# Reordering ScalarE's queue in a fused graph-attention kernel: exp behind the copy of the next transposed weights, part of the norms moved to the attention phase, projection and v adjacent

## Chip, cores and metric

One core of one Trainium2 chip. The metric is the time on the device of one execution, in microseconds (us); each kernel was run several times and the median is quoted. Engines are named as in the profile: PE is TensorE (PEld its weight loads), DVE VectorE, ACT ScalarE, POOL GpSimd, SP SyncE.

## The reference, cut to what matters

The input x is 128 batches of 128 nodes by 512 features, in float32; `adj` is one 128 × 128 matrix used as convolution weight and as attention mask.

```python
# layer 0 (W1 = W2 = adj, so C - A is only b)
A = einsum('od,bdn->bon', adj, x)
pre = A[:, :, None, :] + (C - A)[:, :, :, None]
x = layernorm(x + max(relu(pre), axis=-1))
# layer 1: 8 heads of 64
q, k, v = split(x @ w_qkv)
attn = softmax(where(adj == 0, -inf, q @ k.T * 64**-0.5))
o = (attn @ v) @ w_proj + b_proj
x = layernorm(x + o + layernorm(o) * ln_gamma + ln_beta)
```

## The kernel before

The 128 batches go in 32 groups of 4. A group passes through two phases. In the **dense phase** PE makes eight pieces of qkT for the whole group (pieces 4 to 11, twelve matmuls and 2.8 us each, since a float32 product is made of three products of rounded parts), with one projection left over from the group before among them, and then v of its first batch. In the **attention phase** there are four slots, one for each batch. In a slot PE transposes the weights of the group before (ppt), makes the scores of this group (psc), transposes x of the next group (ptx), applies the transposed weights to v (pav), projects, makes another v and convolves x of a later group (pa).

All of it is a list of pairs (place in time, function). Sorted by place, the list gives the order of PE and of ACT by hand; DVE, POOL and the transfers are ordered by the scheduler. A place is therefore no time at which something happens. It only says which instruction is ahead of which in its engine's queue. The code is shortened: `...` marks what is left out, and conditions for the first and last groups are dropped.

```python
ps_1 = pool("ps_1", bufs=4, PSUM)   # 128 x 512 float32 each: ptx, pav, pm/pd, pa
ps_2 = pool("ps_2", bufs=2, PSUM)   # 128 x 1024 float32 each: pp, psc, ppt
...
STARTS = [0.0, 7.3, 17.4, 27.5, 34.8]

def normed(b, u, v, w, z):          # the norms of layer 1 for one batch
    at(u - 14.0, residual, b)       # xb <- x1, by DMA
    at(u - 10.0, residual_beta, b)  # xb += beta, accumulating DMA issued by POOL (L360)
    at(u - 4.0, residual_o, b)      # xb += o,    accumulating DMA issued by POOL (L380)
    at(u, stats, b, 1)              # ACT square (L392), POOL deviation (L398, L399)
    at(v, norm_1, b)                # DVE L412 (o = (o - mean) * gamma), then L385
    at(w, stats, b, 2)              # ACT square, POOL L398, L399, L406
    at(z, norm_2, b)                # ACT L420, then the output
...
    # attention(g, t, starts), one slot
    last(0.0, transpose_e); last(1.0, weights_T)     # ppt, and ACT's copy eT (L336)
    now(0.95, scores); now(2.1, masked); now(3.5, row_max); now(6.3, exps)
    nxt(2.0, transpose_x); nxt(2.5, split_x); nxt(3.3, split_high)
    u += 2.5
    if i and 0 < g:
        projection((g - 1) * G + i - 1, u); u += 2.8
    last(0.0, attend); last(1.0, heads); last(1.7, split_high of o); u += 1.0
    dense_step(g, i + 1, u)                          # v of the next batch
...
    # beside_dense(g, t): what runs beside the dense phase
    for i in range(G):
        at(u + 0.6 + 0.9 * i, add_0, b + i)          # layer 0 of the next group, ACT L186
        at(u + 5.0 + 0.9 * i, stats_0, b + i)
    at(u + 8.7, rstd_0, b, G)                        # POOL
    for i in range(G):
        at(u + 14.0 + 1.5 * i, norm_0, b + i)        # ACT L205
    for i in range(G):
        u = t + 1.0 + 4.5 * i
        normed((g - 2) * G + i, u, u + 3.0, u + 6.0, u + 9.0)
```

Line numbers: what the profile of the kernel before calls L392 (square), L398 and L399 (deviation) is L391, L397 and L398 after the change, and L388 (`nmean`, the negated mean) is L403. The sum of each qkT or v piece is an ACT copy of its main half (L280) and a DVE addition of its rest (L284). In the profile before, the accumulating DMA issues of 256 KB take 6.7 us (L360, from the beta row) and 3.3 us (L380, from o), medians from issue to landing.

Of the kernel before, what the change touches and what calls it, by code (L numbers as in the profile page):

```python
# [12 lines left out]
ALU = mybir.AluOpType  # L13
# [11 lines left out]
def tile_adj_resnorm_d2(  # L25
# [34 lines left out]
    nc = tc.nc  # L60
    B, T, D = x.shape
    P = 128
    assert T == P and D == 512 and B % 4 == 0
    G = 4
    NG = B // G
# [169 lines left out]
    def split_high(key):  # L235
        nc.scalar.copy(*hs.pop(key))  # L236
# [138 lines left out]
    def projected_rest(b):  # L375
        add_sum(b, 1, pps.pop(("o", b))[1], 1.0, os[b])
# [5 lines left out]
    def add_sum(b, n, in0, scalar, in1):  # L382

        s = sums_of[b, n] = small.tile([P, 3], FP, tag=f"sum{n}", name=f"sum{n}_{b}")
        nc.vector.scalar_tensor_tensor(  # L385
            os[b], in0, scalar, in1, op0=ALU.mult, op1=ALU.add, accum_out=s[:, 0:1],
        )
        nc.gpsimd.tensor_scalar(s[:, 2:3], s[:, 0:1], -1.0 / D, None, op0=ALU.mult)  # L388

    def squares(x, s):  # L390

        nc.scalar.activation(  # L392
            square, x, AF.Square, bias=s[:, 0:1], scale=-float(D), accum_out=s[:, 1:2],
        )

    def deviation(s, n):

        nc.gpsimd.tensor_scalar(s, s, float(D) ** -3, EPS, op0=ALU.mult, op1=ALU.add)  # L398
        nc.gpsimd.tensor_tensor(s, s, mhalf[:, :n], op=ALU.pow)  # L399

    def stats(b, n):
        s = sums_of[b, n]
        squares(os[b], s)  # L403
        deviation(s[:, 1:2], 1)
        if n == 2:
            nc.gpsimd.tensor_tensor(s[:, 2:3], s[:, 2:3], s[:, 1:2], op=ALU.mult)  # L406

    def norm_1(b):
        o, s, xb = os[b], sums_of.pop((b, 1)), xbs.pop(b)
        if b >= B - G:  # L410
            nc.vector.tensor_tensor(xb, xb, o, op=ALU.add)
        nc.vector.scalar_tensor_tensor(  # L412
            o, o, s[:, 2:3], gamma_sb, op0=ALU.add, op1=ALU.mult,
        )
        add_sum(b, 2, o, s[:, 1:2], xb)
# [10 lines left out]
    def at(place, f, *a):  # L426
        plan.append((place, len(plan), f, a))
# [3 lines left out]
    DENSE = (2 * KC + 2) * CHUNK  # L431
    PERIOD = DENSE + STARTS[-1]

    def normed(b, u, v, w, z):

        at(u - 14.0, residual, b)
        at(u - 10.0, residual_beta, b)
        at(u - 4.0, residual_o, b)
        at(u, stats, b, 1)
        at(v, norm_1, b)  # L440
        at(w, stats, b, 2)
        at(z, norm_2, b)

    def projection(b, u):
        at(u, project, b)
        at(u + 1.9, projected_main, b)
        at(u + 2.8, projected_rest, b)
        at(u - 5.0, bias, b)

    def attention(g, t, starts):  # L450

        for i in range(G):
            u = t + starts[i]
            now, last, nxt, far = (
                (lambda place, f, *a, k=k: at(u + place, f, (g + k) * G + i, *a))
                if 0 <= g + k < NG else (lambda *a: None)
                for k in (0, -1, 1, 2)
            )
            last(0.0, transpose_e)
            last(1.0, weights_T)  # L460
            now(0.95, scores)
            now(2.1, masked)
            now(3.5, row_max)
            now(6.3, exps)
            nxt(2.0, transpose_x)
            nxt(2.5, split_x)
            nxt(3.3, split_high)
            u += 2.5
            if i and 0 < g:
                projection((g - 1) * G + i - 1, u)  # L470
                u += 2.8
            last(0.0, attend)
            last(1.0, heads)
            last(1.7, lambda b: split_high(("o", b)))
            u += 1.0
            if 0 < g != NG - 1 and i < G - 1:
                dense_step(min(g, NG - 1), i + 1, u)
                u += 2.8
            far(-20.0, load_x)
            far(0.0, conv)  # L480
            far(1.0, conv_max)
            if NG - 1 <= g:
                v = u + 8.9 if g == NG else u + 12.5 + 2.0 * i
                normed((g - 1) * G + i, v, v + 1.5, v + 3.1, v + (8.6 if g == NG else 5.6))
                now(10.0, weights)

    def dense_step(g, j, u):
        at(u, dense, g, j)
        at(u + 1.9, dense_main, g, j)
        at(u + CHUNK, dense_rest, g, j)  # L490
# [5 lines left out]
    def beside_dense(g, t):  # L496

        if g + 1 < NG:
            b = (g + 1) * G
            u = t if g else t + 19.5  # L500
            at(u + 0.5, relu_0, b, G)
            for i in range(G):
                at(u + 0.6 + 0.9 * i, add_0, b + i)
                at(u + 5.0 + 0.9 * i, stats_0, b + i)
            at(u + 8.7, rstd_0, b, G)
            for i in range(G):
                at(u + 14.0 + 1.5 * i, norm_0, b + i)
                at(u + 15.0 + 1.5 * i, keep_0, b + i)
        for i in range(G):
            if g > 0:  # L510
                at(t + 6.0 + 3.0 * i, weights, (g - 1) * G + i)
            if g > 1:
                u = t + 1.0 + 4.5 * i
                normed((g - 2) * G + i, u, u + 3.0, u + 6.0, u + 9.0)


    for b in range(G):
        at(-20, load_x, b)
        u = -15 + 1.75 * b
# [23 lines left out]
    t = 0.0  # L543
    for g in range(NG):
        beside_dense(g, t)
        if g == 0:
            dense_steps(g, range(3 * KC), t)
            t += 3 * KC * CHUNK
            attention(g, t, (0.0, 4.5, 9.0, 13.5))
            t += 18.0  # L550
            continue
        chunks = [*range(G, 3 * KC)]
        dense_steps(g, chunks[:1], t)
        t += CHUNK
        if g > 1:
            projection((g - 1) * G - 1, t)
            t += CHUNK
        dense_steps(g, chunks[1:], t)
        t += len(chunks[1:]) * CHUNK
        if g < NG - 1:  # L560
            dense_step(g, 0, t)
            t += CHUNK
            attention(g, t, STARTS)
            t += STARTS[-1]
        else:

            attention(g, t, (0.0, 3.6, 10.0, 16.4))
            t += 22.8
            dense_step(g, 0, t)
            projection(g * G - 1, t + CHUNK)  # L570
            t += 2 * CHUNK
            attention(NG, t, (0.0, 6.0, 15.0, 24.0))
            projection(B - 1, t + 32.0)
# [35 lines left out]
```

## Time and profile before

| | before |
|---|---|
| median of three runs | 2138.18 us (2135.07 to 2140.66) |
| span of the profiled run | 2148.1 us |
| mean granted PE clock in it | 0.986 |
| PE waits psc for qkT | 50.0 us, 31 times: once in each of groups 2 to 30, twice in group 31 |
| period of a usual group (from its piece 4 to that of the next) | 65.2 us (median of groups 2 to 29); 66.9 to 67.5 in the six of them in which the clock was lower for a while |

How to read it: an engine that is 96% busy, as PE is here, sets the end, so only the places count where it stands still. The waits of PE give those places by the tile it wanted and the instruction that released it. From there one goes back along the timeline, from releaser to releaser, until an engine is found that did not wait for data but for its own order. The lines are in the prediction below.

### The profile page before, as it was taken

What the parts mean: (1) busy time and instruction counts of PE and PEld (TensorE: products, weight loads), DVE (VectorE), ACT (ScalarE), POOL (GpSimd) and SP (SyncE); (2) the same over time, 40 slices, a digit from 0 to 9 for tenths busy, and PEclk for the clock granted to TensorE, in tenths of its full rate; (3) what the DMA queues carried; (4) which work ended last, traced back from release to release, by engine and by line L of the source; (5) the groups of instructions that cost most, each with busy time, mean ns of one, the idle gap of its engine ahead of it and who ended that gap; (6) DMA issues with size and microseconds to landing.
All of it is one profiled execution on the core that took longest, in us unless ns stands there. A gap on an engine that the chain in (4) does not pass through costs nothing. (4 is left out here: it accounts for less than half of the span.)

```text
span 2148.1 us, 34985 instructions
## 1 busy us (share of the span) xinstructions
PE 2059.5 (96%) x12033; PEld 1602.7 (75%) x12033; DVE 1623.6 (76%) x2615; ACT 1453.9 (68%) x4130; POOL 640.8 (30%) x1329
## 2 busy tenths in 40 slices
PE   7899999999999999999999999999999999999987
PEld 5677777777777777777777777777777777777765
DVE  7788777787777887777877678876778777788767
ACT  5766676765776666767667666667676677666665
POOL 2122333322333222333223332223332233322335
PEclk8999999999999999999999999999999999999998
DMA  6224555334554345554345443454543455434444
GB/s 183 76 62 114 128 128 124 89 93 123 128 128 107 87 110 128 125 128 102 85 118 126 125 117 87 103 128 123 127 100 81 121 128 128 113 79 100 114 102 115
DMA packets 134434, 240.65 MB, mean 112 GB/s; under 512 B 14704, under 2 KB 18928, under 8 KB 134256
## 3 DMA queue, kind: packets, MB, share of 16 engines
q1 hardware_dynamic: 97680, 172.27, 26.3%
q0 software_dynamic: 36288, 66.08, 18.4%
q8 instruction: 95, 1.56, 0.3%
q14 instruction: 83, 0.68, 0.1%
q10 hardware_dynamic: 288, 0.07, 0.0%
HBM read 138.74 MB, written 67.11 MB: 96 GB/s over the span
## 5 line engine op out<-in xcount | busy, mean ns | idle before, releaser
L317 ACT ACTIVATE e<-e,nmax 128x128 f32<-128x128 f32 x1024 | 396.4, 389 | 47.5 <-DVE nmax L310 47.5
L388 POOL TENSOR_SCALAR sum<-sum 128x1 f32<-128x1 f32 x256 | 68.8, 269 | 1109.3 <-DVE o L385 1109.2
L420 ACT ACTIVATE o<-o,sum 128x512 f32<-128x512 f32 x128 | 104.2, 814 | 198.7 <-POOL sum L406 198.4
L236 ACT CAST x_h<-xh 128x512 fp32r<-128x512 f32 x128 | 79.3, 621 | 225.9 <-DVE xh L224 225.5
L399 POOL TENSOR_TENSOR sum<-sum,mhalf 128x1 f32<-128x1 f32 (+1 forms) x291 | 206.5, 710 | 24.1
L295 PE MATMUL psc<-qkT 64*128 64x128 f32 x2048 | 157.6, 288 | 50.0 <-DVE qkT L284 50.0
L336 ACT COPY eT<-ppt 128x1024 f32<-128x1024 f32 x128 | 128.9, 1007 | 100.9 <-PE ppt L332 100.9
L412 DVE SCALAR_TENSOR_TENSOR o<-o,sum,gamma_sb 128x512 f32<-128x512 f32 x128 | 97.0, 758 | 129.5 <-ACT square L392 123.9
L392 ACT ACTIVATE square<-o,sum 128x512 bf16<-128x512 f32 x256 | 182.5, 713 | 14.7 <-DVE o L385 12.8
L317 ACT ACTIVATION_READ_ACCUMULATOR e<-e,nmax 128x1 f32 x1024 | 192.1, 188 | 0.0
L295 PEld LDWEIGHTS psc<-qkT 64*128 64x128 f32 x2048 | 127.1, 187 | 79.2 <-DVE qkT L284 56.2
L385 DVE SCALAR_TENSOR_TENSOR o<-o,sum,xb 128x512 f32<-128x512 f32 x128 | 96.0, 750 | 107.0 <-POOL sum L399 106.8
L302 DVE SCALAR_TENSOR_TENSOR e<-psc,mask 128x1024 f32<-128x1024 f32 x128 | 156.2, 1220 | 13.7 <-PE psc L295 13.7
L332 PEld LDWEIGHTS ppt<-ident,e 128*128 128x128 f32 x1024 | 120.6, 142 | 51.7 <-issue 46.7
L326 DVE TENSOR_TENSOR e<-e,sums 128x1024 f32<-128x1024 f32 x128 | 155.9, 1219 | 1.0
L310 DVE TENSOR_REDUCE nmax<-e 128x8 f32<-128x1024 f32 x128 | 154.6, 1208 | 0.0
L360 POOL DMA_DIRECT2D xb<-in_L_gnn_ln_beta_dram x128 | 125.1, 981 | 82.8 <-DMA xb<-x 69.3
L345 PE MATMUL pav<-eT,v 128*64 128x128 f32 x2048 | 144.4, 285 | 1.1 <-ACT eT L336 1.1
L345 PEld LDWEIGHTS pav<-eT,v 128*64 128x64 f32 x2048 | 112.4, 139 | 42.0 <-issue 40.3
L398 POOL TENSOR_SCALAR sum<-sum 128x1 f32<-128x1 f32 (+1 forms) x291 | 90.4, 311 | 159.3 <-ACT square L392 144.5
L170 PE MATMUL pa<-xt,adjT 128*128 128x512 f32 x256 | 135.3, 615 | 0.4 <-DVE adjT L99 0.4
L332 PE MATMUL ppt<-ident,e 128*128 128x128 f32 x1024 | 133.7, 274 | 0.0
(4778 smaller groups left out, 5570.7 us busy)
## 6 DMA issues: line engine op xcount, KB each, us to landing
xt<-in_x_dram SPq DMA_DIRECT2D x128, 256.0 KB, 2.7
x<-xt SPq DMA_DIRECT2D x128, 256.0 KB, 3.7
xb<-x SPq DMA_DIRECT2D x128, 256.0 KB, 3.2
xb<-in_L_gnn_ln_beta_dram POOLq DMA_DIRECT2D x128, 256.0 KB, 6.7
o<-in_L_gnn_b_proj_dram SPq DMA_DIRECT2D x128, 256.0 KB, 3.7
out_dram<-o SPq DMA_DIRECT2D x128, 256.0 KB, 3.7
xb<-o POOLq DMA_DIRECT2D x124, 256.0 KB, 3.3
wraw<-in_L_gnn_w_qkv_dram SPq DMA_DIRECT2D x12, 256.0 KB, 4.4
```

What stands on the lines that cost most here:

```text
L170: nc.tensor.matmul(pa[b], adjT, xs[b], start=True, stop=True)
L295: nc.tensor.matmul(psc[:, s, hp, :], qkT[hs, hp, i, :], qkT[hs, KC + hp, i, :], start=True, stop=True,)
L302: nc.vector.scalar_tensor_tensor(e, pscs.pop(b).rearrange("p s a m -> p (s a) m"), scale, mask_b, op0=ALU.mult, op1=ALU.add,)
L310: nc.vector.tensor_reduce(nmax, es[b], AX.X, ALU.max, negate=True)
L317: nc.scalar.activation(e[:, j, :], e[:, j, :], AF.Exp, bias=nmax[:, j : j + 1], accum_out=sums[:, j : j + 1],)
L326: nc.vector.tensor_tensor(e, e, sums[:, :, None].to_broadcast([P, H, P]), op=ALU.mult)
L332: nc.tensor.transpose(ppts[b][:, j, :], e[:, j, :], ident)
L336: nc.scalar.copy(eTs[b], ppts.pop(b))
L345: nc.tensor.matmul(pavs[b][s * HD : (s + 1) * HD, hp, :], v[:, h * HD : (h + 1) * HD], eT[:, s * HP + hp, :], start=True, stop=True,)
L360: nc.gpsimd.dma_start(xbs[b], row(ln_beta), accum_op=ALU.add)
L392: nc.scalar.activation(square, x, AF.Square, bias=s[:, 0:1], scale=-float(D), accum_out=s[:, 1:2],)
L399: nc.gpsimd.tensor_tensor(s, s, mhalf[:, :n], op=ALU.pow)
```

## The change

The intent is to even out ACT's queue. There are five parts: (1) the small POOL operation `nmean` goes behind the square; (2) each batch's exp goes behind ACT's copy eT of the next slot; (3) attend goes ahead of the projection, so that projection and v are adjacent; (4) the layer-0 norms of the next group go later, two of the four into the attention phase; (5) the layer-1 norms are spread out, those of a group's fourth batch partly into the attention phase. ACT's small copies `split_high` shift a little with (2) and (3).

```diff
-        nc.gpsimd.tensor_scalar(s[:, 2:3], s[:, 0:1], -1.0 / D, None, op0=ALU.mult)   # in add_sum
...
         squares(os[b], s)                                                             # in stats
+        nc.gpsimd.tensor_scalar(s[:, 2:3], s[:, 0:1], -1.0 / D, None, op0=ALU.mult)
...
-            now(6.3, exps)
+            now((8.5, 11.3, 11.6, 9.0)[i] if 0 < g < NG - 1 else 6.3, exps)
-            nxt(3.3, split_high)
+            nxt(3.3 if i == 3 else 5.0, split_high)
             u += 2.5
+            if g < NG - 1:
+                last(0.0, attend)
+                u += 1.0
             if i and 0 < g:
                 projection((g - 1) * G + i - 1, u)
                 u += 2.8
-            last(0.0, attend)
-            last(1.0, heads)
-            last(1.7, lambda b: split_high(("o", b)))
-            u += 1.0
+            ... (the last groups keep the old place of attend)
+            last(0.1, heads)
+            last(0.8, lambda b: split_high(("o", b)))
...
             for i in range(G):
-                at(u + 0.6 + 0.9 * i, add_0, b + i)
-                at(u + 5.0 + 0.9 * i, stats_0, b + i)
-            at(u + 8.7, rstd_0, b, G)
+                v = u if g == 0 else u + 3.8
+                at(v + 0.6 + 0.9 * i, add_0, b + i)
+                at(v + 5.0 + 0.9 * i, stats_0, b + i)
+            at(u + 8.7 if g == 0 else u + 12.7, rstd_0, b, G)
             for i in range(G):
-                at(u + 14.0 + 1.5 * i, norm_0, b + i)
+                v = u + (14.0 + 1.5 * i if g == 0 else (17.0, 21.0, DENSE + 4.0, DENSE + 12.0)[i])
+                at(v, norm_0, b + i)
...                                                # keep_0 (a transfer) moves along
-                u = t + 1.0 + 4.5 * i
-                normed((g - 2) * G + i, u, u + 3.0, u + 6.0, u + 9.0)
+                u = t + (3.0, 7.5, 12.0, DENSE + 2.0 if g < NG - 1 else 16.0)[i]
+                normed((g - 2) * G + i, u, u + 3.5, u + 7.0, u + 10.5)
```

## The prediction

> **What bounds the kernel now.** I began with the page: busy time by engine, to see which engine can set the end.
>
> ```profile
> PE 2059.5 (96%) x12033; PEld 1602.7 (75%) x12033; DVE 1623.6 (76%) x2615; ACT 1453.9 (68%) x4130; POOL 640.8 (30%) x1329
> ```
>
> TensorE (PE) is busy 96%; only time in which it stands still can be won by reordering. So next I read who PE waited for (total us, times, longest us):
>
> ```profile
> PE psc L295 <- DVE qkT L284: 50.0, 31, 3.2
> PE ptx L216 <- ACT xt L205: 8.4, 4, 2.9
> PE pp_(1, 4)_699 L249 <- ACT x_h L236: 6.5, 1, 6.5
> ```
>
> One wait counts: 50.0 us in 31 pieces, one in each of groups 1 to 31 (the other rows are the start-up). The scores of a group's first batch wait for the last piece of qkT. Why it is late shows in the timeline around that place in group 15, from which I cut the lines that hold each other up:
>
> ```profile
> 1019.09 1.87 POOL L360 DMA_DIRECT2D xb<-in_L_gnn_ln_beta_dram  x2 [2.26 <-DMA xb<-x]
> ...
> 1021.94 0.19 POOL L406 TENSOR_TENSOR sum<-sum 128x1 f32<-128x1 f32 x1
> 1022.17 0.81 ACT L420 ACTIVATE o<-o,sum 128x512 f32<-128x512 f32 x1 [3.19 <-POOL sum L406]
> 1022.89 0.57 ACT L280 ACTIVATE qkT<-pm_(15, 11)_9737 128x512 f32<-128x512 f32 x1
> ...
> 1023.50 0.69 DVE L284 TENSOR_TENSOR qkT<-qkT,pd_(15, 11)_9738 128x512 f32<-128x512 f32 x1 [3.79 <-ACT qkT L280]
> ...
> 1024.24 0.49 PE L295 MATMUL psc<-qkT 64*128 64x128 f32 x4 [2.29 <-DVE qkT L284]
> ```
>
> Bottom up: PE waits for VectorE's sum, that for ScalarE's (ACT) copy, which stands behind the fourth batch's final norm (L420), which waits for GpSimd's (POOL) L406, which stands behind two DMA issues waiting for data. Matmuls of piece 11 had ended near 1017.3; ACT reached it 5.6 us later only by its order. The twelve score matmuls before the wait start at 1021.02; at .068 us each the other four were due at 1021.84, so 2.40 us is lost where the idle column says 2.29: loss is idle + 0.11.
>
> [...] ACT stood 3.19 us in front of L420 with a copy ready behind it. [...] Here it is order instead in the old gap; but buffers come into my second step. [...] a VectorE op of 0.68 us is followed 0.60 us later. I therefore add steps between starts, not durations. [...] the trace has 3.2 us from issue to landing for xb<-x, and I use that.
>
> **The change part by part.** Instructions and counts stay the same; only order moves. Built, the two programs have equal numbers of rows on every engine.
>
> *Removed: the late qkT.* In ACT's built order the fourth batch's statistics, final norm and two of four first norms (norm_0) leave the projection phase for the attention phase. Behind piece 10 stands only the third batch's final norm, then piece 11. I chained this by old durations from the start of the last attention slot (0). POOL issues the first beta DMA at 17.5 and, 5.3 us later (as 1001.98 to 1007.27), may go on: norm_0's statistics to 25.3, the next issue to 26.3, the third batch's first statistics to 27.3; so its L385 ends at 28.0, its buffer is loaded again by 31, issue to 32, and L398, L399, L406 (1.1 us) end at 33.1. Then L420 to 33.9, the copy of piece 11 to 34.4, VectorE's sum to 35.1. PE wants it at 37.4 (1057.50 - 1050.47 = 7.03 from the slot's start to the first piece, and 1021.84 - 991.49 = 30.35 from there to the scores). Slack 2.3 us. I take this wait as gone in groups 2 to 30: 45.2 us idle + 29 × 0.11 = 48 us back. Groups 1 and 31 held 1.2 and 3.6 us; part of it goes too, I say 3 us.
>
> *Added: VectorE in the first attention slot.* The built order puts L412 of the moved batch directly ahead of the masking of the first scores, in each of groups 2 to 29 that I sampled. L412 overwrites what the square reads, so it waits for the square; the square now stands in ACT's order behind the copy eT. And PE's second convolution matmul (pa, L170) needs the PSUM buffer that holds ptx until L226 has read it (four buffers, so the fourth allocation back). These steps are in the old timeline:
>
> ```profile
> 1024.78 1.23 DVE L302 SCALAR_TENSOR_TENSOR e<-psc,mask 128x1024 f32<-128x1024 f32 x1
> 1025.92 0.68 DVE L224 TENSOR_SCALAR xh<-ptx 128x512 int32<-128x512 int32 x1
> 1026.52 1.21 DVE L310 TENSOR_REDUCE nmax<-e 128x8 f32<-128x1024 f32 x1
> 1027.64 0.68 DVE L226 TENSOR_TENSOR x_l<-ptx,xh 128x512 fp32r<-128x512 f32 x1
> ...
> 1029.18 1.02 PE L170 MATMUL pa<-xt,adjT 128*128 128x512 f32 x2
> ```
>
> From the start of the transposes (ppt): eT starts at +1.13 (as at 1040.25 to 1041.38), square +2.14, L412 +2.98 (square's start + 0.84), mask +3.65, L224 +4.79, L310 +5.39, L226 +6.51, its end +7.19, pa +7.25. PE alone would be there at +6.6 (ptx +2.06, pav +2.65, pa 3.93 after pav as at 1025.25 to 1029.18). **New wait 0.65 us**.
>
> In the next slot VectorE is still behind: L227, the head split, L385 of the moved batch (+0.67), v and the maximum end at +11.38, so the mask starts there, and L226 ends at +14.92. The v matmul (pm) that reuses that ptx buffer was due at +14.57 (slot start 8.10 + 6.47, as 1030.03 to 1036.50). **New wait 0.40 us**. By the third slot VectorE is on time again (20.91 against 20.90). Sum 1.05 × 29 groups = 30 us given back.
>
> *Moved at no cost: attend ahead of the projection.* It needs eT at once, 0.5 us after it is ready instead of 3 us. With exp behind eT, ACT is free by then. Slot 1: the head's xh ends at +7.79, then oh, x_h and the v copy, some 0.5 each, end at 9.33, where the transposes end at 8.10 + 1.13 = 9.23. Slot 2: eT to 10.34, exp 3.08, square, norm_0, x_h and L420 to 16.2, oh and v to 18.4, against 19.85. Without the exp move the 3.08 us of exp would stand in front. The switch pauses of PE (0.17 us around pav) number two per slot in either order. *nmean moved on POOL* (0.2 us each, L388): beside other work; it takes POOL's head-of-line wait for VectorE off a few places.
>
> Sum: -48 - 3 + 30 = **-21 us**, 2138 - 21 = 2117 us, 1.0% faster.
>
> **The rivals.**
> 1. *All of it is won.* The new waits are too small to see: 2138 - 53 = 2085 us, 2.5% faster. For it: ACT and VectorE have idle time enough, 32% and 24%. Against: in the attention phase VectorE's work per slot adds to 9.6 of 10.2 us (mask 1.14, row maximum 1.12, weights 1.25, two splits 3.6, projection 1.28, v and maximum 1.2), and the L412 chain holds no estimate but old durations.
> 2. *The old wait stays, smaller.* POOL now takes its L380 ahead of the norm_0 statistics; L380 waits for the beta DMA (6.7 us to land). ACT's norm_0 then stands near 25.4 and everything behind it slips; another 2.3 us and the slack is gone. With half the old loss left: 2117 + 24 = 2141 us, the same. For it: L360's waits total 82.8 us now. Against: the fourth norm's whole chain has left the phase.
> 3. *eT late.* ACT in slot 1 has 0 to 0.1 us of slack before eT, PE some 0.4. If ACT is 1 us later there, attend waits about 0.5 us × 29 = 15 us: 2132 us.
> 4. *TensorE's clock.* Groups with a granted clock of 0.97 take about 67 us, those with 1.00 about 65. Busier PE could bring more such groups; 3 more are 6 us. I know of nothing in the trace that ties them to the change.
>
> **Range and chances.** The size hangs on the two new waits (0.5 to 1.5 us a group, so 15 to 44 us) and on whether the old one is really gone. From 2099 (new waits of 0.45 us) to 2135 (rival 3, or a third of the old wait left). Faster by over 2% needs 2095.4 or less, so nearly rival 1: 0.12. Slower by over 2% needs both rivals 2 and 3 and more: 0.03. The rest, 0.85, within 2%.
>
> **What would show it.** In the waits of PE, "psc from DVE qkT" falls from 50.0 to under 10 us; a row "pa from DVE x_l" appears with some 19 us in about 29 pieces, and "pm from DVE x_l" with about 12. "ACT o L420 from POOL L406" falls from 198.4. In the timeline L412 stands between the v sum and the mask, ended by the square. Busy times stay within 1%. A usual group period goes from 65.0 to about 64.4 us. Wrong I am if pa does not wait (then rival 1), if psc still waits over 1 us a group (rival 2), or if pav waits for eT (rival 3).

## The result, and the profile after

After the change the median is 2109.64 us (four runs, 2107.67 to 2111.54); the kernel before, run in the same rounds on the same chip, has 2139.42 us (2135.07 to 2143.51). The ratio is 0.9861, with a 95% interval of 0.9838 to 0.9884, so 1.4% faster. Here and below a ratio is the mean time of one kernel's fast runs over that of the other's fast runs of the same rounds, so it is not quite the ratio of the medians quoted. All results were correct.

| | before | after |
|---|---|---|
| span of the profiled run | 2148.1 us | 2108.8 us |
| mean granted PE clock | 0.986 | 0.992 |
| PE waits psc | 50.0 us, 31 times | 2.7 us, 2 times |
| PE waits pa in the first slot | none | 11.7 us in 28 pieces |
| ACT waits o (L420) for POOL | 198.4 us | 147.7 us |
| usual group period | 65.2 us | 64.3 us |

The busy times of the page after:

```profile
PE 2053.4 (97%) x12033; PEld 1599.1 (76%) x12033; DVE 1613.3 (77%) x2615; ACT 1458.4 (69%) x4130; POOL 734.8 (35%) x1329
```

The counts are those of before. PE's busy time fell by 6 us though it did the same work. The clock alone takes off 14 us (below). Against that, some 15 us of the new waits count as busy in this column (an estimate: 26.7 us lost, 11.7 shown as idle). POOL's rose by 94 us, 72 of them on the moved `nmean` (L388 with 269 ns each before, L403 with 550 ns after).

The waits of PE after the change (us in total, times, longest us), with two of the many pa rows of one piece each:

```profile
PE psc L295 <- DVE qkT L284: 2.7, 2, 1.8
PE pav L345 <- ACT eT L336: 2.1, 2, 1.1
...
PE pa L170 <- PE pd_(15, 1)_9801 L252: 0.6, 1, 0.6
...
PE pa L170 <- PE pd_(3, 1)_2205 L252: 0.4, 1, 0.4
```

The old wait is gone. Small new ones at pa stand in its place, each on a row of its own because each names another releaser. The timeline after, from the end of a dense phase into the first slot, in group 14 (start, duration, engine and line, idle time ahead of it and releaser):

```profile
940.84 0.81 ACT L420 ACTIVATE o<-o,sum 128x512 f32<-128x512 f32 x1 [1.24 <-POOL sum L406]
...
941.56 0.58 ACT L280 ACTIVATE qkT<-pm_(14, 11)_9083 128x512 f32<-128x512 f32 x1
...
942.17 0.69 DVE L284 TENSOR_TENSOR qkT<-qkT,pd_(14, 11)_9084 128x512 f32<-128x512 f32 x1 [1.85 <-ACT qkT L280]
942.49 1.03 PE L332 MATMUL ppt<-ident,e 128*128 128x128 f32 x8
...
943.46 1.16 PE L295 MATMUL psc<-qkT 64*128 64x128 f32 x16
943.57 1.01 ACT L336 COPY eT<-ppt 128x1024 f32<-128x1024 f32 x1 [0.94 <-PE ppt L332]
944.47 0.73 ACT L391 ACTIVATE square<-o,sum 128x512 bf16<-128x512 f32 x1
...
945.32 0.75 DVE L412 SCALAR_TENSOR_TENSOR o<-o,sum,gamma_sb 128x512 f32<-128x512 f32 x1 [1.86 <-ACT square L391]
...
945.99 1.22 DVE L302 SCALAR_TENSOR_TENSOR e<-psc,mask 128x1024 f32<-128x1024 f32 x1
...
948.85 0.68 DVE L226 TENSOR_TENSOR x_l<-ptx,xh 128x512 fp32r<-128x512 f32 x1
...
949.63 1.10 PE L170 MATMUL pa<-xt,adjT 128*128 128x512 f32 x2 [0.40 <-PE pd_(14, 1)_9168 L252]
```

The upper half is what was won: the copy of piece 11 (941.56) still stands behind an L420, the third batch's, but that one comes early enough. DVE's sum is done at 942.86, and the sixteen score matmuls run as one block, where before the last four stood apart. The lower half is the price. The masking of the scores (945.99) stands behind L412 of the moved batch, which waited 1.86 us for the square, which stood behind eT. Everything of DVE behind it is late, and L226 ends at 949.53. Then pa starts, at 949.63. The profile names `pd` as the releaser. In the built program pa also waits on the semaphore of L226, whose end fits the start to 0.1 us.

### The profile page after: what moved, and what is told of

It is laid out like the page before. It is cut to its first block, busy times and chain, and to the rows that moved or that the text cites. A ratio compares the mean times of both kernels' runs of the same rounds, so it can differ in the third digit from the quotient of the medians.

```text
span 2108.8 us, 35003 instructions
## 1 busy us (share of the span) xinstructions
PE 2053.4 (97%) x12033; PEld 1599.1 (76%) x12033; DVE 1613.3 (77%) x2615; ACT 1458.4 (69%) x4130; POOL 734.8 (35%) x1329
## 3 DMA queue, kind: packets, MB, share of 16 engines
q1 hardware_dynamic: 97680, 172.27, 25.2%
## 5 line engine op out<-in xcount | busy, mean ns | idle before, releaser
L380 POOL DMA_DIRECT2D xb<-o x124 | 112.9, 910 | 686.9 <-DVE o L385 593.5
L420 ACT ACTIVATE o<-o,sum 128x512 f32<-128x512 f32 x128 | 104.0, 813 | 148.2 <-POOL sum L406 147.7
L398 POOL TENSOR_TENSOR sum<-sum,mhalf 128x1 f32<-128x1 f32 (+1 forms) x291 | 198.2, 681 | 22.3
L403 POOL TENSOR_SCALAR sum<-sum 128x1 f32<-128x1 f32 x256 | 140.8, 550 | 169.1 <-DVE o L385 167.1
L360 POOL DMA_DIRECT2D xb<-in_L_gnn_ln_beta_dram x128 | 118.8, 928 | 203.8 <-DMA xb<-x 185.6
L412 DVE SCALAR_TENSOR_TENSOR o<-o,sum,gamma_sb 128x512 f32<-128x512 f32 x128 | 95.9, 749 | 100.1 <-ACT square L391 95.3
L397 POOL TENSOR_SCALAR sum<-sum 128x1 f32<-128x1 f32 (+1 forms) x291 | 106.9, 368 | 187.5 <-ACT square L391 174.1
L302 DVE SCALAR_TENSOR_TENSOR e<-psc,mask 128x1024 f32<-128x1024 f32 x128 | 156.1, 1219 | 3.9 <-PE psc L295 3.9
L310 DVE TENSOR_REDUCE nmax<-e 128x8 f32<-128x1024 f32 x128 | 154.7, 1209 | 0.0
L295 PE MATMUL psc<-qkT 64*128 64x128 f32 x2048 | 150.3, 286 | 2.8 <-DVE qkT L284 2.7
```

What stands on the lines that cost most here:

```text
L295: nc.tensor.matmul(psc[:, s, hp, :], qkT[hs, hp, i, :], qkT[hs, KC + hp, i, :], start=True, stop=True,)
L302: nc.vector.scalar_tensor_tensor(e, pscs.pop(b).rearrange("p s a m -> p (s a) m"), scale, mask_b, op0=ALU.mult, op1=ALU.add,)
L310: nc.vector.tensor_reduce(nmax, es[b], AX.X, ALU.max, negate=True)
L398: nc.gpsimd.tensor_tensor(s, s, mhalf[:, :n], op=ALU.pow)
L403: nc.gpsimd.tensor_scalar(s[:, 2:3], s[:, 0:1], -1.0 / D, None, op0=ALU.mult)
```

## The experiments

The theory was this. The removed psc wait is worth about 50 us in the profile. The moved fourth norm makes two new waits, through L412 ahead of the mask, worth about 1.0 us a group. What the prediction missed is the clock of PE, which drops to half for 3.4 us (a half-clock window) after some of the old waits (then argued, and settled only from the clock records at the end). The rivals: that the exp and attend parts do the work; that the new waits come from the moved layer-0 norms or from attend; that the clock has nothing to do with the waits; and that the whole difference is one of chips or runs.

### Both kernels again

Each has one comment line added and is otherwise the same.

> The kernel before, unchanged, for a profile on the chip of the other three runs (in the first set of experiments it took 2156 us where the case's own runs have 2139). Theory A: what differs from chip to chip is how often the half-clock windows of 3.4 us (1.71 us lost each) fall on the waits; so time, corrected by 1.71 us for each window in the profile, is within 4 us of the same correction of the first profile (2148.1 with ten windows, 2131). Rival: the period without such windows differs between the two profiles by over 0.15 us a group.

> The changed kernel, unchanged, on the same chip as the parts. 2110 us (2105 to 2116), at most one half-clock window between groups 2 and 30, period 64.3 us. If the difference from chip to chip comes from those windows, this time is the same here as in the case's own runs, whatever the kernel before takes.

Measured: before 2149.08 us (2144.9 to 2154.76), against 2153.13 us of the kernel before in the same rounds, ratio 0.9991 (0.995 to 1.0032). After 2112.02 us (2110.18 to 2113.42), ratio 0.9818 (0.9788 to 0.9847). Corrected for their half-clock windows, the two profiles of the kernel before are 2118.2 us long (first chip) and 2118.7 us (here), and their usual periods 65.2 and 65.1 us, so Theory A held and the rival did not. On this chip the kernel before took 10 to 14 us more than on the first, and the changed one 2.4 us more. So the gain is real, and about 1.4% to 1.8%, by the chip. The kernel before also scatters more (10 us against 3 us). Each run of this chip has its mean granted clock recorded: 0.985 to 0.991 for the kernel before, 0.991 to 0.993 for the changed one. The mean of time × clock, which is the time at an equal full clock if PE sets the time throughout (the clock has three digits, so it is good to about 1 us), is 2121.5 us for the kernel before (2121.5 too where it ran again, and 2122.4 to 2123.4 on three more chips) and 2095.0 us for the changed kernel (2094.3 on the first chip). So at an equal clock the change is worth 26.5 us on this chip. The kernel before has nearly the same such time on the four chips where its clock is recorded, so what differs from chip to chip is the clock.

### The fourth norm moved further

This keeps the whole change but puts the layer-1 norms of each fourth batch later in the attention phase, so that L412 is no longer ahead of the first mask.

```diff
+                if i == G - 1 and g < NG - 1:
+                    u = t + DENSE
+                    normed((g - 2) * G + i, u + 4.0, u + 12.5, u + 15.5, u + 20.0)
+                    continue
                 u = t + (3.0, 7.5, 12.0, DENSE + 2.0 if g < NG - 1 else 16.0)[i]
```

> The changed kernel with the fourth batch's norm moved on, so that L412 stands behind the first slot's splits instead of ahead of its mask, and L385 behind the second slot's x_l. Theory A (the change gave back 1.0 us a group by two VectorE waits, 0.65 at pa and 0.35 between projection and v of the next slot): both go, 29 x 1.0 = 29 us off 2110, so 2081 us (2074 to 2090), group period 63.3 us. Rival B (these 1.0 us are not VectorE's order, but the cost of the new order of TensorE itself): the time stays at 2110 and the period at 64.3.

Measured: 2085.38 us (2083.53 to 2086.62), the kernel before 2155.78 us, ratio 0.9671 (0.9656 to 0.9685). The usual period is 63.4 us. Its waits of PE, where no pa row is left in the attention phase:

```profile
PE psc L295 <- DVE qkT L284: 3.1, 2, 1.8
```

And its timeline at the same place of group 14:

```profile
938.09 0.68 DVE L226 TENSOR_TENSOR x_l<-ptx,xh 128x512 fp32r<-128x512 f32 x1
...
939.62 1.02 PE L170 MATMUL pa<-xt,adjT 128*128 128x512 f32 x2
```

L226 now ends 0.85 us ahead of pa, and pa has no idle time. The steps that had grown in the changed kernel are short again: first v 2.90 us (3.47 in the changed kernel), o-projection of the second slot 2.91 (3.16), second v 2.80 (2.88). So the new waits come from L412 at that place and are worth 64.3 - 63.4 = 0.9 us a group.

### Filling the old wait with work

This is the kernel before with the first score products of each group's first batch (four matmuls in the trace) repeated five times ahead of the wait. The result stays right. PE then works where it had stood idle, and the late qkT stays as it was.

```diff
     for hp in range(HP):
         ... (the two score matmuls)
+        if hp == HP - 2 and i == 0 and 0 < g < NG - 1:
+            for _ in range(5):
+                ... (the two score matmuls of hp 0 again)
```

> The kernel before, with ten score matmuls of the group's first batch done again (some 1.36 us, same result) just ahead of the four that wait, in groups 1 to 30: the wait is filled, not removed, and nothing gets ready sooner. Theory A (TensorE's granted clock falls to 0.5 for some 3.4 us after some of these waits, about 2 us each in 8 of 31 groups, because it stood still): the low windows go, mean clock 0.986 to about 0.993, time 2139 to 2128 us (2122 to 2133). Rival (the low windows have nothing to do with the idle time): clock stays at 0.986, time 2139 to 2143 us.

Measured: 2149.52 us (2147.34 to 2154.77), the kernel before 2155.78 us, ratio 0.9977 (0.9956 to 0.9997). Its waits of PE:

```profile
PE psc L295 <- DVE qkT L284: 17.2, 30, 2.8
```

The visible wait fell from 50.0 to 17.2 us, and the time hardly moved, as it must if the path goes through ACT and DVE. The mean granted clock rose from 0.986 to 0.992. Of half-clock stretches (see below) only one is left in the middle of the run, where before there were seven. The gain of 6 us is about half of what I had expected, and the time lies above the expected range, which was counted from 2139 us on the first chip. Time × clock tells the parts: the timed runs went from 0.985 to 0.991, worth some 14 us, while at an equal clock the kernel got slower by 8 us (2123.4 to 2131.5). Of these, 1.1 us is in group 1, which had no wait to fill; the rest I haven't traced. The clock does follow the wait.

### Without the exp move

The changed kernel with part (2) of the exp undone.

```diff
-            now((8.5, 11.3, 11.6, 9.0)[i] if 0 < g < NG - 1 else 6.3, exps)
+            now(6.3, exps)
```

> The changed kernel with exp at its old place. Theory A: attend follows the transposes at once, so exp (3.08 us) of the first batch in front of the second slot's eT makes attend wait about 2.6 us a group: 2110 + 75 = 2185 us (2160 to 2205), and a row of TensorE waiting for ScalarE's eT of about 75 us in some 29 pieces. Rival (moving exp matters little, the norms are the gain): within 10 us of 2110.

Measured: 2218.42 us (2217.95 to 2219.86), ratio to the kernel before 1.0289 (1.0274 to 1.0305). The waits of PE, and one of these waits in the timeline:

```profile
PE pav L345 <- ACT eT L336: 78.8, 31, 4.0
```

```profile
527.85 1.30 PE L345 MATMUL pav<-eT,v 128*64 128x128 f32 x16 [2.54 <-ACT eT L336]
```

The place is the expected one: attend now needs eT at once, and the exp of 3.08 us stands ahead of it. But the time lies above the expected range. The stretch behind that wait shows why; the columns are the stretch, its length, the busy time and count of PE, PEld, DVE, ACT and POOL, the granted PE clock, the DMA share and GB/s:

```profile
528.00:532.00 4.00, 4.00 (x23) 3.09 (x22) 2.48 (x4) 3.98 (x13) 1.16 (x4) 0.57 0.74 175
```

PE is busy all the time but at a little over half of its clock. Nearly every group has such a stretch. The timed runs' clock was 0.972 against 0.985, so of the 62.9 us lost to the kernel before, some 30 are the clock's. So exp has to move **if** attend moves. It is no gain in itself.

### Without the norm moves, and with them alone

First, the changed kernel with parts (4) and (5) undone, then the kernel before with parts (4) and (5) alone. The edits are the last two hunks of the change, reversed and applied.

> The changed kernel without the moved norms: exp behind eT, attend ahead of the projection, the negated mean behind the square. Theory A: the fourth batch's norm still stands in front of the last qkT copy, so the old wait stays at about 1.5 us a group and no new one comes: the time of the kernel before, within 10 us (2130 to 2160 by chip). Rival (ScalarE's evened order in the attention phase is what gains): at least 20 us faster than before.

> The kernel before with the moved norms only: exp, attend, projection and the negated mean as before. Theory A: the old wait of 1.56 us goes, the wait at pa (0.65) comes; exp stands in front of eT, but the projection ahead of attend covers 3 us, so attend is just in time: 2110 us (2103 to 2122). Rival (the gain needs the whole reordering): 2125 us or more.

Measured without the norm moves: 2303.74 us (2299.97 to 2312.11), ratio 1.0715 (1.0675 to 1.0754). I had expected the time of before, which was wrong. Its timeline shows a case that neither the theory nor the rival had:

```profile
1066.88 0.72 ACT L186 ACTIVATE xt<-xt,rm 128x512 f32<-128x512 f32 x1 [4.45 <-POOL rm L180]
```

and its waits of ACT and of PE:

```profile
ACT xt L186 <- POOL rm L180: 136.9, 31, 5.0
```

```profile
PE psc L295 <- DVE qkT L284: 41.0, 25, 2.7
...
PE pp_(15, 10)_9717 L249 <- DVE qkT L284: 2.4, 1, 2.4
```

With the exp of the fourth slot moved later, `add_0` (L186) at its old place stands in ACT's queue ahead of that exp, and it waits 4.45 us for POOL. In 29 groups PE now also waits ahead of piece 10 (72 us in all), beside the old psc wait. So parts (2) and (4) belong together; this run doesn't isolate the norm moves, and the period went to about 70.5 us.

Measured with the norm moves alone: 2112.70 us (2111.13 to 2113.03), ratio 0.9797 (0.9782 to 0.9811), period 64.3 us, pa waiting 0.41 us a group. The ratio is no worse than that of the whole change (0.9861 and 0.9818 on two other chips), and the times at an equal clock agree within about 2 us (2096.5 against 2094.3 and 2095.0). So the exp, attend and nmean parts together add nothing that is seen; none of them was tried alone.

### One of the norm moves at a time

The kernel before with part (5) alone, then the changed kernel with part (5) undone, then the kernel before with part (4) alone.

> The kernel before with one line of the change, the places of the four batches' second norms (fourth batch in the attention phase); first norms, exp, attend and negated mean as before. Theory A: this line alone takes the old wait away and brings the waits of the first two slots: 2112 us (2104 to 2122), period 64.3 us. Rival (the moved first norms are needed too, as ScalarE has 1.4 us more in front of the copy): waits of psc for qkT of over 0.5 us stay, 2122 us or more.

> The changed kernel with only the line of the second norms set back (fourth batch in the projection phase again); first norms, exp, attend and negated mean stay moved. It tells whether the 7% loss of no_norm_move came from the first norms' old place: there ScalarE's add of the next group stood in front of the last exp and waited for the maximum. If so, that loss goes. Theory A then: the fourth norm stands in front of the last qkT copy again, wait of psc for qkT of 0.8 to 1.8 us a group and some half-clock windows, no wait at pa: 2140 us (2120 to 2155). Rival (first norms out of the phase are enough to free the copy): 2090 us or less, as neither old nor new wait is there.

> The kernel before with only the first norms of the next group moved (their adds 3.8 later, two of the four norms into the attention phase); the fourth batch's second norm stays in the projection phase, exp, attend and negated mean stay. In the built order of GpSimd the fourth batch's statistics then stand ahead of the beta DMA that they stood behind. Theory A' (either of the two norm moves frees the last qkT copy; the other parts do nothing): 2083 us (2076 to 2092), period 63.3 us, no wait of psc in groups 2 to 30. Rival (in all_but_fourth it was the exp or attend move that helped): a wait of psc for qkT of 0.8 us or more a group, 2110 us or more.

| kernel | median, us | range | before, us | ratio (95%) | usual period |
|---|---|---|---|---|---|
| before + (5) | 2111.76 | 2111.5 to 2112.95 | 2153.13 | 0.9818 (0.9789 to 0.9847) | 64.3 |
| after without (5) | 2083.12 | 2082.25 to 2084.61 | 2154.45 | 0.9678 (0.9662 to 0.9693) | 63.3 |
| before + (4) | 2086.78 | 2084.34 to 2089.69 | 2149.27 | 0.9702 (0.9685 to 0.9718) | 63.3 to 63.9 |

The second row overturned my theory that the fourth norm has to leave the dense phase. Its timeline in group 18, where that norm is at the old place:

```profile
1183.93 0.20 POOL L406 TENSOR_TENSOR sum<-sum 128x1 f32<-128x1 f32 x1
...
1184.15 0.82 ACT L420 ACTIVATE o<-o,sum 128x512 f32<-128x512 f32 x1
...
1184.88 0.57 ACT L280 ACTIVATE qkT<-pm_(18, 11)_11630 128x512 f32<-128x512 f32 x1
...
1186.29 1.16 PE L295 MATMUL psc<-qkT 64*128 64x128 f32 x16
...
1187.20 0.91 POOL L360 DMA_DIRECT2D xb<-in_L_gnn_ln_beta_dram  x1 [3.08 <-DMA xb<-x]
```

L406 is now ahead of the DMA issue that waits 3.08 us for its data, where in the kernel before it stood behind it. So L420 doesn't wait, and the copy of piece 11 is 1.4 us ahead of the scores. Moving the first norms alone (third row) leaves little of the old wait, where none was expected; half of it is one wait of 3.3 us:

```profile
PE psc L295 <- DVE qkT L284: 6.6, 11, 3.3
```

Part (5) alone does it as well, but it brings the new waits (pa with 11.2 us in 28 pieces). Either move frees the copy. Making both, as the change does, costs about 1 us a group against the first norms alone.

### The fourth norm late, and nothing else

The kernel before with only the hunk of "the fourth norm moved further" added.

> The kernel before with one thing changed: the fourth batch's second norm in the attention phase, with L412 behind the first slot's splits and L385 behind the second slot's x_l (as in late_fourth); nothing else of the change. Theory A (only the place of this norm matters, and exp may stay in front of eT as long as the projection is ahead of attend): 2085 us (2078 to 2095), period 63.4 us. Rival (the rest of the change adds something once the new waits are gone): 2095 us or more.

Measured: 2081.76 us (2080.37 to 2083.12), the kernel before 2154.45 us, ratio 0.9672 (0.9653 to 0.9691), period 63.3 us. This is the fastest of all, with one edit of four lines. Its waits of PE:

```profile
PE psc L295 <- DVE qkT L284: 3.5, 1, 3.5
```

Its difference from "after without (5)" is 1.4 us in the same rounds, with ranges that overlap, and from "moved further" 3.6 us on another chip, so I don't rank these three; all are at 0.967 to 0.968 of before.

## Why the prediction was right or wrong

**What bounds, and why the wait goes: right.** The psc wait fell from 50.0 to 2.7 us. The prediction had DVE's sum ready 2.3 us ahead of need; in group 14 it ends at 942.86, where the last four scores start at 944.23, so 1.4 us ahead. The slack was smaller than worked out, and enough. That the moved fourth norm is the cause was too narrow: moving the first norms does it too, by another order on POOL (group 18 above). The prediction followed one chain through and didn't ask whether a part of the change would do alone.

**The new waits: right in size and in place.** The chain, counted from the start of ppt at 942.49 in group 14:

| step | predicted | measured |
|---|---|---|
| eT starts | +1.13 | +1.08 |
| square | +2.14 | +1.98 |
| L412 | +2.98 | +2.83 |
| mask (L302) | +3.65 | +3.50 |
| L224 | +4.79 | +4.64 |
| L310 | +5.39 | +5.24 |
| L226 | +6.51 | +6.36 |
| pa | +7.25 | +7.14 |

PE's own time between the starts of its stages, in group 14 of before and after, gives the loss: first v and pa together +0.65 us (predicted 0.65), the second slot +0.35 (predicted 0.40), the third +0.02, the fourth nothing. The sum is 1.00 us a group against 1.05. The run with the fourth norm moved further took 0.9 of it back. The usual period is 64.31 us, where 64.4 was predicted.

**The rows foretold: partly wrong.** A row "pa from DVE x_l" with 19 us was announced. There are 28 pieces with 11.7 us, put down to PE's own `pd`; 0.40 us of idle time is shown where 0.65 is lost. "pm from DVE x_l" with 12 us doesn't appear at all: that loss is hidden in longer stages (second-slot projection 3.16 instead of 2.97 us, its v 2.88 after 2.89, ptx 0.59 instead of 0.41). A small wait of a pipelined PE was not read well from the idle column; the distance between the starts of its stages was. "Busy times within 1%" fails for POOL, +94 us, most of it on `nmean`: it was counted with 0.2 us and takes 0.55 us at the new place. Spans on POOL are rough, and no wait of PE is seen to come from it.

**Rivals 1 to 3.** Rival 1 (all of it won) is not this kernel, but it is the kernel before with the fourth norm late: at an equal clock 2064.6 us against 2123.4 on the same chip, 59 us less, where rival 1 gave 53. Rival 2 (half the wait stays, because L380 stands ahead on POOL) did not come: L380 did wait more (80.2 us for the beta DMA, before 23.9), and the slack carried it. Rival 3 (eT late) did not come either: pav's waits sum to 2.1 us. It is what happens without the exp move, there with 2.54 us a group.

**The sum: the sizes that were off.** To take the clock out, I subtracted half of every half-clock stretch from the times of both traces and compared the group periods, the stage of the first scores apart from the rest. The spans then are 2118.2 and 2092.9 us, so 25.2 us apart where 21 were predicted:

| term | predicted, us | measured, us |
|---|---|---|
| old wait, groups 2 to 30 | -48 | -52.7 |
| its part in groups 1 and 31 | -3 | -0.4 |
| new waits (predicted in 29 groups; found in 28, groups 2 to 29) | +30 | +26.7 (1.0 in a usual group) |
| the rest: group 30, start-up and end | 0 | +1.2 |
| sum | -21 | -25.2 |

The largest miss is "loss is idle + 0.11". In group 15 the stage of the first scores took 3.65 us, where without a wait it takes 1.09, so 2.55 us were lost for 2.29 us of idle time, 0.16 more than idle + 0.11; in 29 groups that is some 4.5 us. A third of it is the step "at .068 us each": in the changed kernel the thirteenth matmul starts 0.77 us after the first, not 0.82. The rest is that the last four take 0.42 us to the next stage after a wait, and 0.32 without one. The waits were also put down to the wrong groups: group 1 has none, group 31 two (0.4 and 3.2 us), and the 1.2 us belong to group 2. So groups 2 to 30 held 46.4 us of idle time, not 45.2. Against that, 1.5 us of the wait are left after the change, in groups 7 and 15.

**The clock: the term that was left out.** The step that failed is rival 4: "I know of nothing in the trace that ties them to the change", with nothing of it in the sum. The traces do tie it, and in the other direction. In the kernel before, the timeline has this wait in group 7:

```profile
502.74 0.49 PE L295 MATMUL psc<-qkT 64*128 64x128 f32 x4 [2.46 <-DVE qkT L284]
```

and stretches of a few us behind it show the granted clock (the columns as above; the clock is the third from the right):

```profile
502.00:505.00 3.00, 2.26 (x25) 1.65 (x25) 3.00 (x4) 1.35 (x2) 0.00 (x0) 0.91 0.91 195
505.00:508.00 3.00, 3.00 (x9) 2.44 (x8) 3.00 (x6) 1.16 (x2) 0.00 (x0) 0.52 0.42 154
508.00:512.00 4.00, 4.00 (x32) 3.04 (x30) 2.51 (x5) 3.61 (x18) 0.00 (x0) 1.00 0.31 101
```

PE runs at half its clock for a while, then in full again. In the two profiles of before and after, the trace's clock records give every such stretch as 3.413 us or a multiple of it (up to 13.653 us; only the last one of each run is cut off by the end), and within a run all of them start a whole number of times 3.413 us apart; so each 3.413 us of it loses 1.71 us. How much PE stood idle just ahead of them can be read off by laying windows of that length over the matmul records. The count is over these two profiles, from 130 us after the start to 75 us before the end, for windows at full clock:

| PE idle in the window, us | windows, before | followed by a half-clock window | windows, after | followed by a half-clock window |
|---|---|---|---|---|
| under 0.5 | 525 | 0 | 553 | 0 |
| 0.5 to 1.5 | 27 | 0 | 4 | 0 |
| 1.51 to 1.62 | 3 | 0 | 0 | 0 |
| 1.67 to 2.37 | 7 | 7 | 0 | 0 |

So in the profile before, the seven half-clock windows of this part stand directly behind the seven windows in which PE was idle longest. Like waits differed in this: the 2.29 us of group 15 lies across a boundary of these windows, with 1.36 us of idle time in the fuller one, and no half clock followed it; the 2.46 us of group 7 put 1.67 us into one window, and one did. Where the boundaries fall is not the same in each run: one lies 2.73 us after the first instruction in the profile before, and 1.71 us after it in the one after. In the first profile of the kernel before, the half-clock windows come in groups 5, 7, 18, 22, 24, 28 and 31; in the second one, matmuls of v that start 0.43 us apart instead of 0.23 show them in groups 3, 7 and 26. The half-clock windows in the same middle part of the run, and the mean clock of the timed runs:

| kernel | half-clock windows | clock of its timed runs |
|---|---|---|
| before | 7 | not recorded on the first chip |
| before, again | 7 | 0.987 |
| after, and after again | 0, 0 | 0.992 to 0.994, 0.991 to 0.993 |
| before, wait filled | 1 | 0.991 |
| fourth norm moved further | 0 | 0.992 |
| without the exp move | 27 | 0.972 |
| without the norm moves | 31 | 0.963 to 0.969 |

The windows go when the wait goes or is filled with work, and come in nearly every group where a wait of 2.54 us is put in. In the two profiles they account for 14.0 us (29.9 us lost before, 15.9 after, start-up and end included), which with the 25.2 us makes up the 39.2 us between the spans. In the medians of the first chip they did less: a run of 2139 us, at the 2122 us that the kernel before takes at full clock on the other chips, must have had a clock near 0.992 (an estimate, from those two numbers). So of the 29.8 us there, about 27 are the waits and some 3 the clock. On the chip where both kernels ran again the same change gives 41.1 us (2153.1 to 2112.0), 26.5 of them at an equal clock and the rest by the clock. That the forecast of 21 us comes near is therefore partly luck: on the first chip the clock took little in the timed runs, and on the other one the gain is nearly twice the forecast.

**Moved at no cost: right.** Attend ahead of the projection and the nmean move show no wait of their own; the kernel with parts (4) and (5) alone has the time of the whole change at an equal clock, within 2 us.

**What stays open.** Why waits on the first chip were so rarely followed by a half clock in the timed runs, while its profile had seven such windows, isn't known, since the clock of those runs isn't recorded. Most of the 8 us that filling the wait costs at an equal clock has no cause named.

## What to carry to other kernels

When an engine's order is written by hand, an instruction that waits for a slow partner holds up what stands behind it (in group 15 of the kernel before, a DMA issue on POOL waited 2.26 us for its data, ACT then 3.19 us at L420 with the copy of piece 11 behind it, and PE 2.29 us at the scores): look for the copy that PE needs next, and ask what stands ahead of it on ACT, and what stands ahead of that on POOL. Work moved out of the way arrives somewhere, so count the steps of every engine at the new place too; here another place for one norm was worth a further 1.3% (2112.7 us with the norm moves alone, 2085.4 with the whole change and that norm later, in the same rounds). And try the parts of such a change one at a time: two of these each cured the wait, and both together were slower than either the first norms alone or the fourth norm at a better place.
